# A deformable convolution on one core: window tiles of 4 by 4 pixels become 2 by 8, and five of nine sampling weights travel through DRAM as two factors

## The chip, the cores and the metric

The kernel runs on one core of a Trainium2 chip. The core has a matrix engine (TensorE, PE in the profile), a vector engine (VectorE, DVE), a scalar engine (ScalarE, ACT), a general engine (GpSimd, POOL) and a sequencer that issues transfers (SyncE, SP). Transfers run on sixteen DMA engines that SP and ACT both feed. The metric is the device time of one execution in microseconds (us). Everything is float32.

## The reference

The input is x[2, 128, 128, 128] (image, channel, row, column). Four layers are added up in a residual stream; the third of them is the one that changes. It is a deformable 3 by 3 convolution with 128 input and 128 output channels on the normalised stream g:

```
off, mask = conv3x3(g, w_off) + b_off      # 9 taps: (dy, dx) and sigmoid(mask) for each pixel
py = dy + ky + h - 1 ; px = dx + kx + w - 1
sampled[c, k, h, w] = mask * bilinear(g[c], py, px)     # four neighbours, zero outside
out[o, h, w] = sum_{c,k} w_def[o, c, k] * sampled[c, k, h, w] + b_def[o]
```

A bilinear sample is a sum over window positions (y, x) of `hat(py - y) * hat(px - x) * g[c, y, x]` with `hat(t) = relu(1 - |t|)`. So a sample is a product of a row factor and a column factor, and it can be done as a matrix product of the window's pixels with these weights.

## The kernel before

The program is one long unrolled stream. `program` runs an attention layer (`layer0_prepare`, `layer0_attention`, `layer0_merge`), four recurrent scans (`layer1`), the deformable layer (`layer2`) and a Winograd convolution (`layer3`). The change touches `layer2` alone.

`layer2_offsets` goes over 16 blocks of 16 rows. For each it normalises the stream, computes the 27 offset and mask channels with the matrix engine, turns them so that pixels lie on partitions, and sends them to the DRAM buffer `off`; it also turns the normalised image so that columns lie on partitions and sends it to the DRAM buffer `px`, which has a border of zeros. At the end it tests whether an offset is over 2 in size. If none is, `layer2_windows` runs, and that is the case here.

`layer2_windows` cuts the image into 128 halves: four rows (`RT = 4`) by 64 columns. A half has 16 tiles of 4 by 4 pixels, done in two batches of eight tiles (128 pixels), so there are 256 batches. Here a half, or in the new kernel a strip, is called a pair of batches.

- `load` fetches for each half the window of each tile, 10 by 10 positions, with positions on partitions and channels along the free dimension: `xw[100, 16, 128]`. It takes ten transfers, one for each window row, each to ten partitions, and one more for the offsets `o`. All are issued by SP, and `xw` has four buffers.
- `hats`, `hatted` and `masked` make the row and column hats `d[128 pixels, 2, 18, 10]`: DVE subtracts positions from coordinates, ACT takes the absolute value and the relu, DVE multiplies the row hats with the mask.
- `outer` (DVE) multiplies row and column hats of one batch to `w[128, 9, 10, 10]`. `turn` transposes this on PE, one transpose for each tap, to the PSUM tile `ps_w[100, 9, 128]`, and `turned` (DVE) copies it to `s`, ordered by tile.
- `sample` (PE) multiplies for each of eight tiles the window by the weights of its 9 taps and 16 pixels: 8 products with 144 columns into `ps_s`. `sampled` (ACT) copies this to `sm` with three copies.
- `convolve` (PE) sums nine products of `wdef` with `sm` over the 256 pixels of a half into `po`, five taps in one batch and four in the next. `finish` (DVE) adds `po` and the bias to the stream, and takes the statistics for the next norm after every second half.

Each float32 product runs as two passes on PE, so eight products are 16 matrix instructions in the profile; a transpose is one.

The order is written out by hand. `InOrder` makes PE, DVE and ACT keep the program's order. In iteration `b` of the loop PE does `turn` for batch b+1, `sample` for b, and then the part of `convolve` for the half before; ACT does `sampled` after `sample`. A framework places all waits. It gives every transfer of SP and ACT one of eight semaphores in turn (numbers 100 to 107 in the trace, the two engines share them), and a transfer waits before its issue until the one that last had its semaphore has landed.

Nearly all instructions of the loop are recorded under line 81, the helper `InOrder`; they are told apart by their tiles.

Of the kernel before, what the change touches and what calls it, by code (L numbers as in the profile page):

```python
# [7 lines left out]
F32 = mybir.dt.float32  # L8
# [7 lines left out]
P = 128  # L16
N = 2
# [7 lines left out]
TP = S + 6  # L25
# [1099 lines left out]
def layer2_offsets(env, prm, res, mem, st_gn, far):  # L1125
# [5 lines left out]
    with ExitStack() as ctx:  # L1131
# [7 lines left out]
        zero = cp.tile([P, 402], F32, name="zero", tag="zero")  # L1139
        nc.vector.memset(zero, 0.0)  # L1140
        for n in range(N):
            flat = mem["px"][n].rearrange("y x k -> (y x k)")
            for y in (0, S + 3):
                span = 3 * TP * P
                nc.scalar.dma_start(
                    out=flat[y * TP * P : y * TP * P + span].rearrange("(p k) -> p k", p=P),
                    in_=zero,
                )
            for c in (0, S + 3):
                nc.scalar.dma_start(  # L1150
                    out=mem["px"][n, 3 : S + 3, c : c + 3, :].rearrange("y x k -> y (x k)"),
                    in_=zero[:, 0 : 3 * P],
                )
# [7 lines left out]
        for n in range(N):  # L1161
            for h in range(0, S, NR):
# [15 lines left out]
                for k in range(9):  # L1178
# [9 lines left out]
                om = sp.tile([P, 4, RT, 32], F32, name="om", tag="om")  # L1188
                nc.scalar.activation(
                    om.rearrange("p b r c -> p r b c"),  # L1190
                    ps.rearrange("p r (b c) -> p r b c", b=4),
                    AF.Identity,
                    bias=boff,
                )
# [38 lines left out]
def layer2_windows(env, prm, res, mem, st_next):  # L1233
# [3 lines left out]

    nc, tc = env.nc, env.tc
    ident = env.ident
    with ExitStack() as ctx:  # L1240
# [3 lines left out]
        pe, dve, act = (InOrder(tc, e) for e in (nc.tensor, nc.vector, nc.scalar))  # L1244
# [4 lines left out]
        base = cp.tile([P, 18, 10], F32, name="base", tag="base")  # L1249
        nc.scalar.dma_start(out=base, in_=prm["base2"])  # L1250

        px = mem["px"]
        halves = [(n, g, hf) for n in range(N) for g in range(NT) for hf in range(2)]

        def load(at):
            n, g, hf = halves[at]
            xw = sp.tile([100, 16, P], F32, name="xw", tag="xw", bufs=4)
            for y in range(10):
                here = px[n, g * RT + y, hf * 64 : hf * 64 + 10, :]
                src = bass.AP(  # L1260
                    tensor=here.tensor,
                    offset=here.offset,
                    ap=[[P, 10], [4 * P, 16], [1, P]],
                )
                nc.sync.dma_start(out=xw[10 * y : 10 * y + 10], in_=src)
            o = sp.tile([P, 2, 27], F32, name="o", tag="o", bufs=4)
            nc.sync.dma_start(out=o, in_=mem["off"][n, g, :, 2 * hf : 2 * hf + 2, :])
            return xw, o

        def hats(o):  # L1270
            d = sp.tile([P, 2, 18, 10], F32, name="d", tag="d")
            dve.tensor_tensor(
                d,
                o[:, :, 0:18].unsqueeze(3).to_broadcast([P, 2, 18, 10]),
                base.unsqueeze(1).to_broadcast([P, 2, 18, 10]),
                ALU.add,
            )
            return d

        def hatted(d):  # L1280
            act.activation(d, d, AF.Abs)
            act.activation(d, d, AF.Relu, bias=1.0, scale=-1.0)

        def masked(d, o):
            rows = d.rearrange("p b (k a) s -> p b k a s", a=2)[:, :, :, 0, :]
            dve.tensor_tensor(
                rows, rows, o[:, :, 18:27].unsqueeze(3).to_broadcast([P, 2, 9, 10]), ALU.mult
            )

        def outer(d, b):  # L1290
            w = sp.tile([P, 9, 10, 10], F32, name="w", tag="w")
            v = d[:, b].rearrange("p (k a) s -> p k a s", a=2)
            dve.tensor_tensor(
                w,
                v[:, :, 0, :].unsqueeze(3).to_broadcast([P, 9, 10, 10]),
                v[:, :, 1, :].unsqueeze(2).to_broadcast([P, 9, 10, 10]),
                ALU.mult,
            )
            return w

        def turn(w):
            ps = pp.tile([100, 9, P], F32, name="ps_w", tag="ps_w")
            for k in range(9):
                pe.transpose(ps[:, k, :], w[:, k].rearrange("p y x -> p (y x)"), ident)
            return ps

        def turned(ps):

            s = sp.tile([100, 8, 36, 4], F32, name="s", tag="s")
            dve.tensor_copy(  # L1310
                s.rearrange("p t k c -> p k t c"),
                ps.rearrange("p k (r t c) -> p (k r) t c", r=4, t=8),
            )
            return s

        def sample(xw, s, b):
            ps = pp.tile([P, 3, 512], F32, name="ps_s", tag="ps_s")
            for t in range(8):
                pe.matmul(
                    ps[:, t // 3, (t % 3) * 144 : (t % 3) * 144 + 144],  # L1320
                    lhsT=xw[:, 8 * b + t, :],
                    rhs=s[:, t].rearrange("p k c -> p (k c)"),
                    start=True,
                    stop=True,
                )
            return ps

        def sampled(ps, sm, b):
            for j in range(3):
                nt = (3, 3, 2)[j]  # L1330
                lo = 8 * b + 3 * j
                act.copy(
                    sm.rearrange("p k (t c) -> p k t c", c=4)[:, :, lo : lo + nt, :],
                    ps[:, j, 0 : nt * 144].rearrange("p (t k c) -> p k t c", t=nt, c=4),
                )

        def convolve(sm, po, taps):
            for k in taps:
                pe.matmul(
                    po,  # L1340
                    lhsT=wdef[:, k, :],
                    rhs=sm[:, 4 * k : 4 * k + 4, :],
                    start=(k == 0),
                    stop=(k == 8),
                )

        def finish(at, po):
            n, g, hf = halves[at]
            here = res[n][:, g * RT : g * RT + RT, hf * 64 : hf * 64 + 64]
            dve.scalar_tensor_tensor(here, po, bdef[:, 0:1], here, ALU.add, ALU.add)  # L1350
            if hf == 1:
# [7 lines left out]
        count = len(halves)  # L1359
        loads = {at: load(at) for at in range(3)}  # L1360
        ds = {}
        for at in range(2):
            ds[at] = hats(loads[at][1])
            hatted(ds[at])
            masked(ds[at], loads[at][1])
        w = outer(ds[0], 0)
        ps_w = turn(w)
        s = turned(ps_w)
        w = outer(ds[0], 1)
        sms, pos = {}, {}  # L1370
        for b in range(2 * count + 2):
# [3 lines left out]
            if part == 0 and at < count:  # L1375
                sms[at] = sp.tile([P, 36, 64], F32, name="sm", tag="sm")


            s_now = s
            if b + 1 < 2 * count:  # L1380
                ps_w = turn(w)
                s = turned(ps_w)
                if b + 2 < 2 * count:
                    w = outer(ds[(b + 2) // 2], b % 2)
            if at + 2 < count:
                if part == 0:
                    ds[at + 2] = hats(loads[at + 2][1])
                else:
                    masked(ds[at + 2], loads[at + 2][1])
            if b < 2 * count:  # L1390
                ps_s = sample(loads[at][0], s_now, part)
                sampled(ps_s, sms[at], part)
                if part == 0 and at + 2 < count:
                    hatted(ds[at + 2])
            if at >= 1:
                if part == 0:
                    pos[at - 1] = pp.tile([P, RT, 64], F32, name="po", tag="po_w", bufs=2)
                convolve(sms[at - 1], pos[at - 1], range(0, 5) if part == 0 else range(5, 9))
                if part == 1:
                    finish(at - 1, pos.pop(at - 1))  # L1400
                    sms.pop(at - 1), loads.pop(at - 1), ds.pop(at - 1)
# [336 lines left out]
def program(ctx, tc, prm, out):  # L1738
# [16 lines left out]
    mem["px"] = dram.tile([N, TP, TP, P], F32, name="px_d", tag="px_d")  # L1755
# [21 lines left out]
def constants(np):  # L1777
# [27 lines left out]
    pix = np.arange(P)[:, None, None]  # L1805
    at = np.stack(
        [tap // 3 + 2 + pix[:, 0] // 32, tap % 3 + 2 + pix[:, 0] % 4], 2
    ).reshape(P, 18, 1)
    base2 = (at - np.arange(10)).astype(np.float32)
# [94 lines left out]
```

## Time and profile before

| | |
|---|---|
| three runs | 5779.77, 5784.55 and 5788.11 us, median 5784.55 us |
| profiled execution | 5786.06 us; its span, first to last instruction, 5783.8 us |
| busy in the span | PE 5374.1 us, DVE 3770.7 us, ACT 2638.0 us, POOL 1292.9 us |
| deformable layer, offsets part | 3836 to 4017 us |
| deformable layer, windows part | first load issued at 4024.0 us, first sample 4056.3 us, last addition to the stream ends at 5310.0 us |
| PE busy, 4500 to 5100 us | 600.0 of 600 us, granted clock 1.00 |
| DVE and ACT busy, 4500 to 5100 us | 381.0 and 207.7 us |

A line of the profile names the line of code, the engine, the operation, the tile that is written and those that are read, the number of partitions and elements, and how often it occurs. Then follow busy time and mean duration, and the idle time of the engine just before such instructions with what ended it. Matrix instructions are pipelined: their durations overlap, so the cost of one is the distance between starts. PEld is the loading of weights for the next product, beside PE.

### The profile page before, as it was taken

How to read it: one execution, taken by the hardware profiler on the slowest of the kernel's cores; microseconds unless marked ns; L12 is line 12 of the kernel's file. 1: busy time of each engine (PE TensorE's matmuls, PEld its weight loads, DVE VectorE, ACT ScalarE, POOL GpSimd, SP SyncE). 2: the span in 40 equal slices, each digit the busy share in tenths (PEclk: the TensorE clock that was granted, in tenths of full speed). 3: DMA queues.
4: the chain of work that ended last, by engine and by line, in shares of the span. 5: the costliest groups of instructions: out<-in, count | busy, mean ns of one | idle time of the engine just before them, and what ended most of it. 6: DMA issues, size and time to landing. Idle time of an engine off the chain costs nothing. (4 is left out here: it accounts for less than half of the span.)

```text
span 5783.8 us, 162452 instructions
## 1 busy us (share of the span) xinstructions
PE 5374.1 (93%) x67323; PEld 4833.4 (84%) x67323; DVE 3770.7 (65%) x7273; ACT 2638.0 (46%) x7896; POOL 1292.9 (22%) x983
## 2 busy tenths in 40 slices
PE   8997999999999607999999999997999999998999
PEld 8866888888888407999999999963999999998888
DVE  3645888888888655555555556653666666666887
ACT  1056988899888555442223320012333333333221
POOL 2114666666666420000000013310000000000000
PEclk9998999999999758999999999998999999999999
DMA  3243333333333482000000001114667676773001
GB/s 145 96 190 109 60 58 65 60 59 61 63 60 58 141 316 79 1 2 1 2 1 1 1 9 45 39 60 121 89 88 87 86 87 89 87 90 50 41 37 41
DMA packets 411363, 401.00 MB, mean 69 GB/s; under 512 B 63232, under 2 KB 368256, under 8 KB 397952
## 3 DMA queue, kind: packets, MB, share of 16 engines
q1 hardware_dynamic: 406160, 380.65, 31.5%
q8 instruction: 541, 8.86, 0.7%
q10 hardware_dynamic: 4464, 9.86, 0.5%
q14 instruction: 198, 1.62, 0.1%
HBM read 251.00 MB, written 139.37 MB: 67 GB/s over the span
## 5 line engine op out<-in xcount | busy, mean ns | idle before, releaser
L81 PE MATMUL pl<-ln,wl 128*128 128x128 f32 (+1 forms) x10160 | 1238.5, 276 | 8.1 <-DVE ln L81 8.1
L81 PEld LDWEIGHTS pl<-ln,wl 128*128 128x128 f32 x10160 | 1175.6, 190 | 18.2 <-issue 5.1
L81 ACT ACTIVATE e<-e,mx 128x128 f32<-128x128 f32 x2048 | 793.5, 395 | 1.0 <-DVE mx L81 1.0
L81 ACT COPY sm<-ps_s 128x432 f32<-128x432 f32 (+1 forms) x768 | 318.2, 487 | 797.5 <-PE ps_s L81 797.5
L81 POOL TENSOR_TENSOR e<-e,total 128x1024 f32<-128x1024 f32 x256 | 485.6, 1897 | 481.9 <-DVE total L81 473.6
L81 ACT COPY res<-ln 128x128 f32<-128x128 f32 x762 | 261.8, 344 | 720.5 <-DVE ln L81 720.5
L81 PE MATMUL ps_s<-s,xw 100*128 100x144 f32 x4096 | 545.2, 286 | 0.5 <-ACT sm L81 0.5
L81 DVE COPY s<-ps_w 100x1152 f32<-100x1152 f32 x256 | 346.5, 1353 | 299.8 <-PE ps_w L81 299.8
L81 PE MATMUL po<-sm,wdef 128*128 128x256 f32 x2304 | 539.2, 379 | 0.0
L81 PE MATMUL pl<-ln,ws 128*128 128x128 f32 x4064 | 537.3, 273 | 0.0
L81 POOL COPY et<-et 128x1024 f32<-128x1024 f32 x256 | 518.9, 2027 | 34.9 <-DVE et L81 25.9
L81 PEld LDWEIGHTS ps_s<-s,xw 100*128 100x128 f32 x4096 | 517.2, 190 | 1.1 <-ACT sm L81 1.0
L81 DVE TENSOR_TENSOR v<-pl,c 128x128 f32<-128x128 f32 x508 | 148.2, 292 | 539.5 <-PE pl L81 539.5
L81 PEld LDWEIGHTS pl<-ln,ws 128*128 128x128 f32 x4064 | 495.1, 191 | 0.0
L81 ACT ACTIVATE r<-gen,alphas 128x1536 f32<-128x1536 f32 x256 | 395.0, 1543 | 164.7 <-PE gen L81 140.3
L81 POOL TENSOR_TENSOR res<-ln,x1t 128x128 f32<-128x128 f32 x256 | 134.0, 524 | 1484.4 <-DVE ln L81 1484.4
L81 PEld LDWEIGHTS po<-sm,wdef 128*128 128x128 f32 x2304 | 419.8, 190 | 47.6
L81 PE MATMUL m<-x,weff 128*128 128x256 f32 x2048 | 445.2, 381 | 15.1 <-DVE x L81 15.1
L81 PEld LDWEIGHTS m<-x,weff 128*128 128x128 f32 x2048 | 391.2, 191 | 68.8 <-issue 15.1
L1653 POOL MEMSET col<- 128x10 f32 x32 | 3.7, 116 | 1867.5 <-ACT weff L1633 1488.3
L81 ACT ACTIVATION_READ_ACCUMULATOR e<-e,mx 128x1 f32 x2048 | 396.2, 193 | 0.0
L81 DVE SCALAR_TENSOR_TENSOR ln<-v,res 128x128 f32<-128x128 f32 x1016 | 343.9, 339 | 48.6 <-DVE v L81 0.9
(225 smaller groups left out, 8782.4 us busy)
## 6 DMA issues: line engine op xcount, KB each, us to landing
xw<-px_d SPq DMA_DIRECT2D x1280, 80.0 KB
xa<-in_x SPq DMA_DIRECT2D x16, 1024.0 KB
v_d<-vs SPq DMA_DIRECT2D x16, 1024.0 KB
qb_d<-sb SPq DMA_DIRECT2D x16, 1024.0 KB
qa_d<-sa SPq DMA_DIRECT2D x8, 2048.0 KB
zz<-qb_d SPq DMA_DIRECT2D x1024, 16.0 KB
vt<-v_d SPq DMA_DIRECT2D x64, 256.0 KB
qk<-qa_d SPq DMA_DIRECT2D x256, 64.0 KB
```

The costliest lines, as they stand in the source:

```text
L81: return lambda *a, **k: self.tc.keep_in_program_order(issue(*a, **k))
L1653: nc.gpsimd.memset(cols[0][:, :, 0:1], 0.0)
```

## The change

The windows part takes another cut of the image and another way for the weights of five taps.

- **Tiles.** The 128 units are strips of two rows by 128 columns. A batch is half a strip, 2 by 64 pixels, with eight tiles of 2 by 8 pixels. A window is 8 rows by 16 columns (`WY`, `WX`), so 128 positions (`KW`). `px` gets two more zero columns. The offsets part writes its transposed values in the strip's order, which splits one ACT instruction (`om`) into two.
- **Loads.** A batch's windows come with eight transfers, one for each tile, each to 128 partitions: the four even tiles issued by SP, the four odd tiles by ACT. There are five buffers of one batch each; the loads of batch b+5 are issued after `sampled` of batch b. The offsets are a transfer of their own (`load_offsets`). SP keeps the program's order too.
- **Five taps as factors.** Row and column hats lie in `d` by place (24 places: 8 rows and 16 columns) and tap, five taps first and four after. `hats` takes four DVE instructions and `masked` two. `send` turns the factors of five taps for a whole strip with two transposes (`ps_h`), ACT copies them (`ht`), and SP stores them in a DRAM buffer `hat` with two transfers. `receive` reads them back with two transfers into `hat0` and `hat1`, `[128, 2, 5, 128]` each: the row factors repeated for each of 16 columns, the column factors repeated for each of 8 rows.
- **Four taps as before.** `outer` and `turn` do four taps. `weights` (DVE) fills `s`: a product of `hat0` and `hat1` for five taps, and a copy of `ps_w` for four.
- **Convolution.** `convolve` does all nine taps for 128 pixels of one batch, for the batch before.

```diff
+WX, WY = 16, 8
+KW = WX * WY
+PLACES = WX + WY
+TD = 5
...
+        def load(b):
+            n, g, k = strips[b // 2]
+            y, x = g * RT + 2 * k, b % 2 * 64
+            xw = sp.tile([KW, 8, P], F32, name="xw", tag="xw", bufs=5)
+            for part, queue in enumerate((sync, act)):
+                for t in range(part, 8, 2):
+                    queue.dma_start(
+                        out=xw[:, t, :],
+                        in_=mem["px"][
+                            n, y : y + WY, x + 8 * t : x + 8 * t + WX, :
+                        ].rearrange("y x k -> x y k"),
+                    )
+            return xw
...
+        def send(at, d):
+            ps = pp.tile([PLACES * TD, 2, P], F32, name="ps_h", tag="ps_h")
+            for b in range(2):
+                pe.transpose(ps[:, b, :], d[:, b, 0 : PLACES * TD], ident)
+            ht = sp.tile([PLACES * TD, 2, P], F32, name="ht", tag="ht")
+            act.copy(ht, ps)
+            for b in range(2):
+                sync.dma_start(out=there(at)[:, b], in_=ht[:, b, :])
+
+        def receive(at):
+            got = []
+            src = there(at).rearrange("s b k x -> s (b k x)")
+            for a in range(2):
+                t = sp.tile([KW, 2, TD, P], F32, name=f"hat{a}", tag=f"hat{a}")
+                here = src[0:WY] if a == 0 else src[WY:PLACES]
+                dims = [list(v) for v in here.ap]
+                dims = [[0, WX], dims[0], dims[1]] if a == 0 else [dims[0], [0, WY], dims[1]]
+                sync.dma_start(
+                    out=t.rearrange("p b k x -> p (b k x)"),
+                    in_=bass.AP(tensor=here.tensor, offset=here.offset, ap=dims),
+                )
+                got.append(t)
+            return got
...
+        def weights(got, b, ps):
+            s = sp.tile([KW, 8, 18, 8], F32, name="s", tag="s")
+            to = s.rearrange("p t k c -> p k t c")
+            row, col = (
+                t[:, b].rearrange("p k (r t c) -> p (k r) t c", r=2, t=8) for t in got
+            )
+            dve.tensor_tensor(to[:, 0 : 2 * TD], row, col, ALU.mult)
             dve.tensor_copy(
...
+                to[:, 2 * TD : 18], ps.rearrange("p k (r t c) -> p (k r) t c", r=2, t=8)
             )
             return s
...
+        for b in range(2 * count + 1):
             at, part = b // 2, b % 2
-            if part == 0 and at + 3 < count:
-                loads[at + 3] = load(at + 3)
...
+            if part == 0 and at + 4 < count:
+                offs[at + 4] = load_offsets(at + 4)
             s_now = s
             if b + 1 < 2 * count:
-                ps_w = turn(w)
-                s = turned(ps_w)
+                s = weights(gots[(b + 1) // 2], 1 - part, turn(w))
                 if b + 2 < 2 * count:
-                    w = outer(ds[(b + 2) // 2], b % 2)
...
+                    w = outer(ds[(b + 2) // 2], part)
+            if part == 0 and at + 2 < count:
+                send(at + 2, ds[at + 2])
+            if part == 0 and at + 3 < count:
+                ds[at + 3] = hats(offs[at + 3])
+            if part == 1 and at + 3 < count:
+                masked(ds[at + 3], offs.pop(at + 3))
             if b < 2 * count:
-                ps_s = sample(loads[at][0], s_now, part)
-                sampled(ps_s, sms[at], part)
...
+                ps_s = sample(xws[b], s_now)
+                sms[b] = sampled(ps_s)
+                if part == 0 and at + 3 < count:
+                    hatted(ds[at + 3])
+            if part == 1 and at + 2 < count:
+                gots[at + 2] = receive(at + 2)
+            if b + 5 < 2 * count:
+                xws[b + 5] = load(b + 5)
+            if b >= 1:
+                last, half = (b - 1) // 2, (b - 1) % 2
+                if half == 0:
+                    pos[last] = pp.tile([P, 2, S], F32, name="po", tag="po_w", bufs=2)
+                convolve(sms.pop(b - 1), pos[last][:, :, 64 * half : 64 * half + 64])
+                if half == 1:
+                    finish(last, pos.pop(last))
```

More of the change, by code (lines that the diff above doesn't have):

```diff
@@ L1248, in layer2_windows @@
         nc.scalar.dma_start(out=bdef, in_=prm["bdef"])
-        base = cp.tile([P, 18, 10], F32, name="base", tag="base")
+        base = cp.tile([P, 9 * PLACES], F32, name="base", tag="base")
         nc.scalar.dma_start(out=base, in_=prm["base2"])
[L1252 to L1268, printed above, removed]
@@ L1270, in hats @@
-        def hats(o):
[L1271 to L1277, printed above, removed]
+        hat = mem["hat"]
+        strips = [(n, g, k) for n in range(N) for g in range(NT) for k in range(2)]
+        count = len(strips)
+        def load(b):
[11 more added lines that the diff above has]
+            return xw
@@ new lines, in load_offsets, with parts @@
+        def load_offsets(at):
+            n, g, k = strips[at]
+            o = sp.tile([P, 2, 27], F32, name="o", tag="o", bufs=3)
+            sync.dma_start(out=o, in_=mem["off"][n, g, :, 2 * k : 2 * k + 2, :])
+            return o
+        def parts(t):
+            cut = PLACES * TD
+            return (
+                (t[..., 0:cut].rearrange("... (s k) -> ... s k", k=TD), slice(0, TD)),
+                (t[..., cut:].rearrange("... (s k) -> ... s k", k=TT), slice(TD, 9)),
+            )
@@ new lines, in hats @@
+        def hats(o):
+            d = sp.tile([P, 2, 9 * PLACES], F32, name="d", tag="d", bufs=3)
+            for (to, taps), (less, _) in zip(parts(d), parts(base)):
+                for a, here in ((0, slice(0, WY)), (1, slice(WY, PLACES))):
+                    out = to[:, :, here, :]
+                    dve.tensor_tensor(
+                        out,
+                        o[:, :, a:18:2][:, :, taps].unsqueeze(2).to_broadcast(list(out.shape)),
+                        less[:, here, :].unsqueeze(1).to_broadcast(list(out.shape)),
+                        ALU.add,
+                    )
@@ L1284, in masked, with there @@
         def masked(d, o):
[L1285 to L1288, printed above, removed]
+            for to, taps in parts(d):
+                rows = to[:, :, 0:WY, :]
+                mask = o[:, :, 18:27][:, :, taps].unsqueeze(2).to_broadcast(list(rows.shape))
+                dve.tensor_tensor(rows, rows, mask, ALU.mult)
+        def there(at):
+            n, g, k = strips[at]
+            return hat[:, n * NT + g, 2 * k : 2 * k + 2]
@@ L1347, in finish @@
         def finish(at, po):
[L1348 to L1349 removed]
+            n, g, k = strips[at]
+            here = res[n][:, g * RT + 2 * k : g * RT + 2 * k + 2, :]
             dve.scalar_tensor_tensor(here, po, bdef[:, 0:1], here, ALU.add, ALU.add)
[L1351 removed]
+            if k == 1:
                 dve.bn_stats(
@@ L1355, in finish @@
                 )
-        count = len(halves)
-        loads = {at: load(at) for at in range(3)}
-        ds = {}
+        offs, ds, gots, xws, sms, pos = {}, {}, {}, {}, {}, {}
+        for at in range(3):
+            offs[at] = load_offsets(at)
+        xws[0] = load(0)
+        for at in range(3):
+            ds[at] = hats(offs[at])
+            hatted(ds[at])
+            masked(ds[at], offs.pop(at))
+            if at < 2:
+                send(at, ds[at])
+        offs[3] = load_offsets(3)
@@ L1362, in layer2_windows @@
         for at in range(2):
-            ds[at] = hats(loads[at][1])
-            hatted(ds[at])
-            masked(ds[at], loads[at][1])
+            gots[at] = receive(at)
+        for b in range(1, 5):
+            xws[b] = load(b)
         w = outer(ds[0], 0)
-        ps_w = turn(w)
-        s = turned(ps_w)
+        s = weights(gots[0], 0, turn(w))
         w = outer(ds[0], 1)
-        sms, pos = {}, {}
-        for b in range(2 * count + 2):
+        for b in range(2 * count + 1):
             at, part = b // 2, b % 2
-            if part == 0 and at + 3 < count:
-                loads[at + 3] = load(at + 3)
-            if part == 0 and at < count:
-                sms[at] = sp.tile([P, 36, 64], F32, name="sm", tag="sm")
+            if part == 0 and at + 4 < count:
+                offs[at + 4] = load_offsets(at + 4)
```

106 lines of the change are left out of this document (48 added, 58 removed).

## The prediction

> **What bounds the kernel now.** I read the busy shares first, then the windows part by stretches, then PE's order of work in it, and last what SP's transfers wait for. The stretches (length, then busy time of PE, PEld, DVE, ACT and POOL, then clock, DMA share and GB/s):
>
> ```profile
> 4500.00:4700.00 200.00, 200.00 (x1394) 187.83 (x1393) 126.69 (x153) 69.16 (x164) 0.00 (x0) 1.00 0.67 87
> 4700.00:4900.00 200.00, 200.00 (x1394) 187.76 (x1393) 127.36 (x154) 68.88 (x164) 0.00 (x0) 1.00 0.71 88
> ```
>
> PE is never idle and its clock is full. A pair of batches has 68 matrix instructions (2 x (9 + 16 + 9)), so a pair takes 200 / 1394 x 68 = 9.76 us, and 128 pairs are 1249 us. In order of time:
>
> ```profile
> 4700.17 1.15 PE L81 MATMUL ps_w<-cst_main,w 128*100 128x128 f32 x9
> 4701.15 2.13 PE L81 MATMUL ps_s<-s,xw 100*128 100x144 f32 x16
> 4703.11 2.32 PE L81 MATMUL po<-sm,wdef 128*128 128x256 f32 x10
> 4705.27 1.15 PE L81 MATMUL ps_w<-cst_main,w 128*100 128x128 f32 x9
> ```
>
> The distance between starts is the price: 0.98 us for 9 transposes (109 ns each), 1.96 us for 16 passes of 144 columns (122.5 ns), 2.16 us for 10 passes of 256 (216 ns). What the other engines do, 4300 to 5200 us:
>
> ```profile
> L81 DVE COPY s<-ps_w 100x1152 f32<-100x1152 f32 x184 | 249.0, 1353 | 214.4 <-PE ps_w L81 214.4
> L81 DVE TENSOR_TENSOR w<-d 128x900 f32<-128x900 f32 x184 | 199.8, 1086 | 0.0
> L81 ACT COPY sm<-ps_s 128x432 f32<-128x432 f32 x368 | 173.0, 522 | 570.0 <-PE ps_s L81 570.0
> L81 ACT ACTIVATE d<-d 128x360 f32<-128x360 f32 x184 | 94.5, 514 | 18.3 <-DVE d L81 15.4
> ```
>
> DVE and ACT wait for PE. SP's waits, for the whole run (us in all, times, longest):
>
> ```profile
> SPq L1265 <- PE ps_s L81: 386.9, 115, 5.0
> SPq L1265 <- DMA xw<-px_d: 227.7, 406, 1.4
> ...
> SPq L1265 <- DMA wdef<-in_wdef: 3.2, 1, 3.2
> ```
>
> The first is a buffer coming free. The others are transfers that wait for a transfer with which they share no data: the eight shared semaphores. The third shows that SP waits so for one that ACT issued. Today this costs nothing, because the loads run three halves ahead.
>
> **What the change takes from PE.** Per batch 9 transposes become 4, and `send` adds 2 per strip, so 1: 5 x 109 = 0.55 us for 0.98. `sample` stays 16 x 122.5 = 1.96. `convolve` becomes 18 passes of 128 columns for 9 of 256; the scans' products of that shape start 109 to 112 ns apart, so 1.96 to 2.02 us for 1.94. Together 4.47 to 4.53 us; I take 4.52, or 9.04 a pair. If PE stayed the bound, 128 x (9.76 - 9.04) = 92 us would go. The `pl` rows already show 128 by 128 weights loaded anew for each pass of 128 columns at that distance, so the load lies hidden beside the stream. The Trainium skill ("TensorE: Matmul & The Clock Gate", The mechanism, and LDWEIGHTS) speaks against this half of the change: a weight load overlaps a running product only in another row group, and 128 columns take 128 / 1.2 = 107 ns. By it nine loads more per batch would cost an estimated 0.96 us, 246 us in all, and turn the gain of 92 into a loss of some 154.
>
> **DVE, per pair**, at the rows' 1.04 ns an element plus 0.15 us (900 elements 1.09 us, 360 elements 0.53 us): `outer` 2 x 0.68 for 2 x 1.09; `weights` 2 x (640 elements, 0.82, and a PSUM copy of 512, 0.69 as such a copy takes elsewhere) for 2 x 1.35; `hats` four instructions on 432 elements 1.05 for 0.53; `masked` two, 0.45 for 0.34; `finish` and statistics stay at 0.83. That is 6.7 us beside 9: hidden. Without that cover it would be 0.1 us a pair more than now (6.6).
>
> **ACT, per pair:** the `sampled` copies 2 x 1.24 as now, `hatted` 2 x 0.58 for 432 elements (0.51 for 360), the `ht` copy 0.36 (as 128x256 from PSUM elsewhere), and eight transfers. ACT's transfers of zeros took 0.33 to 0.47 us each to issue: 3.2 us. Sum 7.2 of 9: it fits, but ACT's next copies queue behind each issue, and PE's next `sample` behind these copies (one `ps_s`). The `om` split costs 0.03 us a block: nothing.
>
> **SP, per pair:** thirteen issues (offsets, 2 sends, 2 receives, 8 loads) at 0.40 us, the distance of back-to-back loads now: 5.2 us. The loads move from the head of the iteration to behind `sampled`; being five batches ahead, some 22 us, they are not late by that. POOL issues nothing in this part.
>
> **DMA, per pair.** Now a load goes to ten partitions, and its semaphore gets eleven steps where a transfer to 128 partitions gets sixteen; its 512-byte packets take 53 ns in the median, 27 at best. 1600 of them at about 190 per us, the rate in the first loads, need 8.4 of the 9.76 us. After: 2048 packets of 512 bytes over 16 engines (128 each), 256 of 5,120 bytes (16 each), 240 to `hat`, 128 of offsets. At 27 ns, which the sends of `px` from all 128 partitions also show (28), and 198 ns (4,608 bytes take 178): 128 x 0.027 + 16 x 0.198 + 20 x 0.028 + 0.2 = 7.4 us of 9. At 53 ns for the loads it is 10.7. I take 27 ns as the partitions are those of the sends, and keep 53 for the range. The skill ("DMA: Bandwidth & Descriptors", Why a DMA increments its semaphore by 16 and not by 1) reads the eleven steps as ten engines, by the outer dimensions, and would give the new loads sixteen; it sets no price for a packet, so the sum by it is the same.
>
> **The new round trip.** This decides. Between `receive` of one strip and `send` of the next the program has 13 transfers (12 loads and the offsets), more than the eight semaphores. So one of them waits until `receive` has landed; whether SP or ACT issues it, the next `send` stands behind it (on ACT its `ht` copy does). And `receive` waits for `send` to land, as it reads those bytes. The strips' transfers form one chain, however far ahead `receive` is written. One turn, from the landing of `receive` (0):
>
> - The held load starts at once (17 ns after a landing in this trace), then offsets, first send, second send start at 0.4 us steps: second send at 1.2.
> - It lands 1.9 to 2.4 us later (`sve_d` stores, also 64 KB in 512-byte rows: least 1.87, median 2.37, issue to last semaphore step): 3.1 to 3.6.
> - SP must also issue the next batch's four loads, the first of which wants the semaphore of the held load: about 2.2 (64 KB), plus 4 x 0.4 = 3.8. So `receive` starts at 3.8.
> - Its two reads are 1.31 MB. The nearest single reads: 590 KB (`wl`) land in 3.7 us, 1.05 MB (`x1t`) in 5.1, and the second half adds 8 x 0.198 = 1.6: 5.4 us. Meanwhile ACT's four loads, freed when the sends and two loads land, share the engines: 4 x 8 x 27 ns = 0.85.
> - Sum 3.8 + 5.4 + 0.85 = 10.05 us a pair. Ends: 8.9 (stores 1.9, nothing shared) and 10.9 (everything at its slower row), and 12 if the repeated reads run at 300 GB/s with 53 ns loads beside them.
>
> This is above PE's 9.04 and above today's 9.76, so PE will wait. I take 10.05: 128 x 0.29 = +37 us.
>
> The skill's first fixed cost for a transfer ("DMA: Bandwidth & Descriptors", Anatomy of one DMA) is about 2.0 us plus bytes at 436 GB/s, measured on another queue. By it the turn would be an estimated 3.8 + 5.0 + 0.85 = 9.65, and the change a gain of 24 us with the start.
>
> **Start and end.** PE's first sample comes 32 us after the first load now, since three halves of loads go first. Afterwards: base lands near 4031, hats, relu and mask 2.7, transposes and copy 0.7, sends 2.8, `receive` 5.4, weights 1.5: near 4045. I take 10 us saved; 0 and 13 are the bounds.
>
> **Sum** against the profiled execution's 5786 us (span 5784 and 2 around it, 1.5 above the runs' median): 5786 - 10 + 37 = 5813.
>
> **Rivals.**
>
> 1. *The round trip hides.* If `receive` lands within 5.2 us of its start, sharing included, a turn is 9.04 or less and PE bounds: 5786 - 10 - 92 = 5684. For it: 27 ns packets and a DMA sum of 7.4. Against: no read of 1 MB in this trace landed faster than 4.9. The sign turns at a turn of 9.84 us. Between lies a half gain: through ACT, whose loads wait for the sends and whose copies PE needs, I count 9.4 (send 2.6, loads issued to 5.6, landed 8.5, issue and `ht` copy 0.9): 5786 - 10 - 46 = 5730.
> 2. *DMA becomes the bound.* Packets of 512 bytes stay at 53 ns: 10.7 us of engine time, a turn near 11: 5786 - 10 + 159 = 5935. For it: that is today's median; against: ten partitions explain it.
> 3. *The repeated reads don't use sixteen engines.* On eight, 256 packets of 5,120 bytes take 6.3 us for 3.2, a turn of 13.2: 5786 - 10 + 440 = 6216. Against: the outer dimension is 16 in both.
>
> **How the numbers follow.** Turn 9.7 to 10.6 (5770 to 5885): 0.43. Rival 1 whole: 0.20; half: 0.17. Rival 2: 0.16. Rival 3: 0.04. About 0.2%, 12 us, is what a measurement can tell from no change. Faster is rival 1 and its half, and a little of the first: 0.38; within 0.2% is a turn of 9.75 to 9.93: 0.08; slower 0.54. The range runs from PE's floor, 5682, to 5925, short of rival 2's middle; the likeliest case alone has 5770 to 5885.
>
> **What would show it.** Right: PE with 1 us idle per pair in the windows part, ended by the DVE product that waits for `hat0` or `hat1` from DMA, or by `sm`; SP's loads waiting for `hat0` or `hat1` to land; sends waiting behind; first sample near 4045. Wrong: PE busy through (rival 1); packets of 512 bytes at 50 ns and DMA share near 1 (rival 2); fewer than 16 steps of the receives' semaphores (rival 3). What breaks the forecast most easily is the 5.4 us of two repeated reads, which nothing in this trace resembles.

## The result, and the profile after

The changed kernel takes 6377.3 us (median of 4 runs, 6372.5 to 6383.5), against 5782.2 us before on the same chip: a ratio of 1.1028, 95% interval 1.1009 to 1.1047. It is 10% slower. The forecast was 5813 us and its range ended at 5925: the direction was right, the size was not. The profiled execution has a span of 6373.4 us.

The stretches of the windows part, in the columns of the same view before (length, busy time of PE, PEld, DVE, ACT, POOL, then clock, DMA share, GB/s):

```profile
4300.00:4500.00 200.00, 152.18 (x1098) 149.93 (x1098) 92.59 (x191) 54.34 (x126) 0.00 (x0) 0.86 0.75 176
4700.00:4900.00 200.00, 154.40 (x1078) 152.33 (x1079) 91.67 (x189) 54.34 (x126) 0.00 (x0) 0.85 0.75 174
```

PE was busy for all of the 200 us; now it idles for some 46 of them, and its clock is no longer full. A pair of batches has 78 matrix instructions now (2 x (4 + 1 + 16 + 18)), and the turn, the distance from one strip's `receive` to the next, is 14.43 us in the median. Forecast was 10.05; before, a pair took 9.76. PE in order of time (start, duration, what; in brackets the idle time ahead and what ended it):

```profile
5001.19 2.13 PE L86 MATMUL ps_s<-s,xw 128*128 128x144 f32 x16
5003.15 2.17 PE L86 MATMUL po<-sm,wdef 128*128 128x128 f32 x18
5009.05 1.09 PE L86 MATMUL ps_w<-cst_main,w 128*128 128x128 f32 x4 [3.72 <-DVE d L86]
5009.93 0.63 PE L86 MATMUL ps_h<-cst_main,d 128*120 128x128 f32 x2
5010.35 4.05 PE L86 MATMUL ps_s<-s,xw 128*128 128x144 f32 x16
...
5023.34 0.63 PE L86 MATMUL ps_w<-cst_main,w 128*128 128x128 f32 x4 [2.26 <-DVE d L86]
5023.80 0.38 PE L86 MATMUL ps_h<-cst_main,d 128*120 128x128 f32 x2
5024.02 2.13 PE L86 MATMUL ps_s<-s,xw 128*128 128x144 f32 x16
```

The passes themselves have the forecast's prices: 1.96 us from the start of 16 passes to the next group. What is new are the gaps at the head of a turn, and after the longer one (3.72 us) the passes run at half speed for a while: 16 of them took 4.05 us, and 2.13 after the gap of 2.26. DVE is named as the releaser, but it is late itself, as the second row below shows. What DVE, PE and ACT wait for, 4300 to 5300 us (us in all, times, longest):

```profile
ACT sm L86 <- DMA xw<-px_d: 351.3, 61, 8.4
DVE s L86 <- DMA hat<-hat_d: 309.4, 68, 7.5
...
PE ps_w L86 <- DVE d L86: 245.7, 69, 6.4
...
ACT ht L86 <- DMA xw<-px_d: 180.7, 57, 4.2
```

The second row is a real need: the product that makes `s` wants the hats read back. The first and fourth are not. ACT's copies need no `xw`; they stand behind ACT's own loads, which wait for a semaphore, as ACT in order of time shows:

```profile
5016.18 5.11 ACTq L86 DMA_DIRECT2D xw<-px_d  x4
5021.33 0.52 ACT L86 COPY sm<-ps_s 128x432 f32<-128x432 f32 x1 [4.60 <-DMA xw<-px_d]
```

SP's waits in that stretch (4300 to 5300 us) say the same, the second row once a turn (69 times, 2.5 us each):

```profile
SPq L86 <- DMA xw<-px_d: 224.7, 140, 3.8
SPq L86 <- DMA hat<-hat_d: 171.7, 69, 3.7
```

One turn on SP in order of time (start, duration of all the issues of the row, what, how many):

```profile
5020.94 0.33 SPq L86 DMA_DIRECT2D o<-off_d  x1
5021.59 1.64 SPq L86 DMA_DIRECT2D hat_d<-ht  x2
5023.34 2.49 SPq L86 DMA_DIRECT2D xw<-px_d  x4
5025.94 1.17 SPq L86 DMA_DIRECT2D hat<-hat_d  x2
5027.22 6.35 SPq L86 DMA_DIRECT2D xw<-px_d  x4
```

The `receive` before had landed at 5020.72, and only then does the row of offsets start. The semaphores of the trace tell what held it, the same in all 69 turns from 4300 to 5300 us. SP's fourth load waits for the first read of the `receive`, and ACT's next load for the second. The offsets wait for neither: they want the semaphore of the window load that SP issued 0.7 us behind the second read, and this load lands 0.25 us after that read (medians). What is to be sent, `ht`, had by then been ready for 9 us or more. So the sends wait for semaphores, and not for data.

The two sends take 0.8 us each to issue, the four loads 0.62 each; the next `receive` starts 5.2 us after the landing of the last, and lands at 5035.40, 9.5 us later.

The medians of the turns, without some twenty at the start and ten at the end, make a ledger of two terms:

| from the landing of a `receive` | forecast, us | measured, us |
|---|---|---|
| second send starts | 1.2 | 1.93 |
| second send has landed | 3.1 to 3.6 | 4.25 |
| next `receive` starts | 3.8 | 5.84 |
| the pair of reads, issue to landing | 6.25 | 8.49 |
| turn | 10.05 | 14.43 |

(The medians add up to 14.33; they are taken one by one.) 128 x (14.43 - 9.76) = 598 us, and the start saves 6 (the first `sample` is at 4050.0 us, before at 4056.3): 5786 - 6 + 598 = 6378, against 6375 in the profiled execution. The whole loss lies in the turn. What is to be explained is why both terms are so much longer than forecast.

### The profile page after: what moved, and what is told of

Same layout as the page of the kernel before. It is cut to its first block, busy times and chain, and to the rows that moved or that the text cites. A ratio compares the mean times of both kernels' runs of the same rounds, so it can differ in the third digit from the quotient of the medians.

```text
span 6373.4 us, 167224 instructions
## 1 busy us (share of the span) xinstructions
PE 5519.6 (87%) x68603; PEld 5036.6 (79%) x68603; DVE 3818.5 (60%) x8041; ACT 2701.6 (42%) x8040; POOL 1293.0 (20%) x983
## 5 line engine op out<-in xcount | busy, mean ns | idle before, releaser
L86 PE MATMUL ps_s<-s,xw 128*128 128x144 f32 x4096 | 703.9, 339 | 7.1 <-ACT sm L86 7.1
L86 PEld LDWEIGHTS ps_s<-s,xw 128*128 128x128 f32 x4096 | 680.9, 240 | 7.4 <-ACT sm L86 7.4
L86 PE MATMUL ps_w<-cst_main,w 128*128 128x128 f32 x1024 | 194.5, 323 | 459.4 <-DVE d L86 440.2
L86 PE MATMUL po<-sm,wdef 128*128 128x128 f32 x4608 | 564.5, 277 | 0.0
L86 DVE TENSOR_TENSOR s<-hat,hat 128x640 f32<-128x640 f32 x256 | 211.2, 825 | 584.8 <-DMA hat<-hat_d 565.2
L86 PEld LDWEIGHTS po<-sm,wdef 128*128 128x128 f32 x4608 | 550.6, 195 | 0.0
L86 PEld LDWEIGHTS ps_w<-cst_main,w 128*128 128x128 f32 x1024 | 137.0, 164 | 480.5 <-issue 477.2
```

The costliest lines, as they stand in the source:

```text
L86: return lambda *a, **k: self.tc.keep_in_program_order(issue(*a, **k))
```

## The experiments

The kernel before took 5784 to 5790 us on the chips of these runs. "Landing to next" and "pair" are the two terms of the ledger, in medians of the same turns.

**Which part costs?** The first two runs take the round trip away, with and without the five taps' savings on PE.

Sends and receives for the first two strips alone; the hats are still turned and copied:

```diff
-            for b in range(2):
-                sync.dma_start(out=there(at)[:, b], in_=ht[:, b, :])
+            if at < 2:
+                for b in range(2):
+                    sync.dma_start(out=there(at)[:, b], in_=ht[:, b, :])
...
-                gots[at + 2] = receive(at + 2)
+                gots[at + 2] = gots[at]
```

> Only the first two strips are sent and received; later strips use their factors again, so the weights of five taps are those of other pixels. The transposes and the ht copies stay, four transfers per pair are left out. Theory (the chain through receive and send bounds the part): no chain is left, PE bounds at 9.04 us a pair, 5680 to 5740 us. Rival (ACT's issuing of loads, or the loads themselves, hold PE): over 6000 us.

Measured: 5698.3 us.

```profile
4700.00:4900.00 200.00, 200.00 (x1730) 199.97 (x1729) 145.05 (x297) 86.68 (x202) 0.00 (x0) 1.00 0.43 120
```

PE is busy throughout, at 200 / 1730 x 78 = 9.02 us a pair; ACT still issues its four loads a batch, and PE isn't held up by it. So the new PE work costs what was forecast (9.04), and everything above 5698 us is the round trip with its reads.

The tiles of 2 by 8 and the loads to 128 partitions alone, all nine taps turned on PE:

```diff
-TD = 5
+TD = 0
...
-            if at < 2:
-                send(at, ds[at])
...
-            if part == 1 and at + 2 < count:
-                gots[at + 2] = receive(at + 2)
```

> The tiles of 2 by 8 pixels with their loads on both queues alone: all nine taps are made by outer, turned by nine transposes and copied; send, receive and the factors are left out. Complete computation. Theory: PE bounds at 2 x (9 x 0.109 + 1.96 + 2.0) = 9.9 us a pair, 5770 to 5830 us. Rival (ACT's issuing of loads holds PE): over 6000 us.

Measured: 5804.8 us, PE busy for 600 of 600 us with 5185 instructions, 600 / 5185 x 86 = 9.95 us a pair. The new tiles and loads by themselves hold nothing up and gain nothing.

**Why does the pair of reads take 8.5 us?** In the changed kernel the packets of 512 bytes have a median of 27 ns, as forecast, but those of 5,120 bytes 369 ns (10% at 196, 90% at 404), where 198 was forecast. Three suspects: the places lie 640 KiB apart in DRAM; each place is read 8 or 16 times; the bytes were written a few us before.

The places of a strip 5 KB apart:

```diff
-    mem["hat"] = dram.tile([PLACES, N * NT, 4, TD, P], F32, ...)
+    mem["hat"] = dram.tile([N * NT, 2, PLACES, 2, TD, P], F32, ...)
...
-            return hat[:, n * NT + g, 2 * k : 2 * k + 2]
+            return hat[n * NT + g, k]
```

> One edit: the buffer hat is laid out strip by strip, so that the 24 places of a strip lie 5 KB apart instead of 640 KiB. Theory (one chain per strip: receive lands, the next send, the next receive; its receives are slow in this kernel because their 5,120-byte packets take 369 ns in the median instead of 196). If the distance of the places is what makes them slow: packets near 200 ns, receive pair lands in 5.4 to 6.3 us instead of 8.5, a turn falls from 14.4 to 11.3 to 12.2 us, 5980 to 6095 us in all. If the repetition of the same bytes is what makes them slow: packets stay near 370 ns, and 6350 to 6400 us. Rival (the loads that ACT issues hold its copies and so PE, whatever receive does): 6350 to 6400 us.

Measured: 6336.7 us, a turn of 13.97, landing to next 5.67, pair 8.18, packets of 5,120 bytes 364 ns. The pitch is worth some 41 us of the 595 lost. The Trainium skill ("DMA: Bandwidth & Descriptors", Latency and other measured facts) tells of large power-of-two row pitches, which at 4 MiB cut the rate to about half, with an inferred cause. The pitch here, 640 KiB, is no power of two, and this run shows that another pitch leaves most of the slowness in place (364 ns for 369).

The same number and size of packets to the same partitions, but every partition reads bytes of its own, in `px`:

```diff
-                    in_=bass.AP(tensor=here.tensor, offset=here.offset, ap=dims),
+                    in_=px[lo : lo + KW * 2 * TD * P].rearrange("(p k) -> p k", p=KW),
```

> The two receives read as many bytes in as many packets of 5,120 bytes, but 128 different rows of the buffer px that lie one behind the other, so nothing is repeated; the weights of five taps are then wrong. The sends stay. receive no longer waits for send by its data, but stands behind it on SP all the same. Theory, repeated reads slow: packets near 196 ns, receives land in 5.4 to 6.3 us, a turn of 11.3 to 12.2 us, 5980 to 6095 us. Rival (the volume of the receives beside the loads is what costs, whatever they read): packets stay over 300 ns, 6300 to 6400 us.

Measured: 6112.5 us, just above the theory's range, a turn of 12.28, landing to next 5.43, pair 6.51, packets of 196 ns. This pair is near the forecast's 6.25. But these bytes were also old. So the repetition was put back, still reading old bytes of `px`:

```diff
-                    in_=px[lo : lo + KW * 2 * TD * P].rearrange("(p k) -> p k", p=KW),
+                    in_=bass.AP(tensor=here.tensor, offset=here.offset, ap=dims),
```

Here `here` is 8 or 16 rows of `px`, and `dims` repeats them as in the changed kernel.

> As the run whose receives read different bytes for every partition, with the repetition put back: the receives read the same old tensor px, eight places for 16 partitions each and 16 places for eight partitions each, in the pattern of the changed kernel (the five taps' weights are not theirs). It parts two things that the other run changed at once: there no byte was read twice, and none had been written a few us before. Theory (the repetition itself is slow): 5,120-byte packets of 330 to 380 ns, the pair of receives lands 8.2 us after its issue, a turn of 14.0, near the 6337 us of the buffer laid out strip by strip. Rival (bytes written just before are slow to read, repetition costs nothing): packets of 196 ns, 6.5 us, a turn of 12.3, near 6112 us.

Measured: 6351.1 us, a turn of 14.17, pair 8.28, packets of 365 ns. The repetition is the cause, and the age of the bytes is not. Both reads are slow: of the 256 packets of a turn the first 128 to start, mostly those of the eight rows read by 16 partitions each, take 339 ns in the median, and the others, mostly those of the 16 rows read by eight, 376.

**Why does the next `receive` start 5.8 us after a landing?** The first theory was the one of the forecast: the tie lies in the semaphores that sends and receives share with the loads. So GpSimd, which is idle here and has semaphores of its own, was made to issue them:

```diff
-                sync.dma_start(out=there(at)[:, b], in_=ht[:, b, :])
+                pool.dma_start(out=there(at)[:, b], in_=ht[:, b, :])
...
-                sync.dma_start(
+                pool.dma_start(
                     out=t.rearrange("p b k x -> p (b k x)"),
```

> Sends and receives are issued by GpSimd, idle in this part, whose transfers have eight semaphores of their own; nothing else changes. Theory (the eight semaphores that SP and ACT share tie each send to the landing of the receive before it): the chain is cut, and receives run ahead. What bounds then is PE at 9.04 us a pair or the DMA engines at 16 x 0.37 + 128 x 0.027 + 0.8 = 10.2 us, so 5690 to 5880 us, by the sum 5830. Rival (the repeated reads themselves, or the loads behind them in the same rings, bound a pair): over 6150 us.

Measured: 6305.6 us, a turn of 13.92, landing to next 5.26, pair 8.97. Only 72 us went; the theory fell in this form. The waits of that run, 4300 to 5300 us:

```profile
POOL hat_d L86 <- ACT ht L86: 582.9, 71, 12.1
ACT ht L86 <- DMA xw<-px_d: 284.3, 38, 9.7
```

and SP's own:

```profile
SPq L86 <- DMA xw<-px_d: 422.7, 104, 7.0
```

The send waits for ACT's copy `ht`, and this stands behind ACT's loads. A load that has the DMA engines to itself lands 2.2 us after its issue; one that meets a `receive` lands with it. In this run a quarter of SP's and of ACT's loads take over 7.6 us, and one in twenty over 9.1, though the `receive` is issued by another engine. Eight such loads fill the eight semaphores, SP and ACT stop, and the chain closes again through the loads. The Trainium skill ("DMA: Bandwidth & Descriptors", Issuing engines are not separate DMA queues) has transfers of all issuing engines interleave on the same DMA engines, and says that another issuer saves only the sequencer's time, usually little beside the transfer. The first half agrees with the 2.2 and 7.6 us here. The second did not hold in the run further on that moves four of a batch's eight loads from ACT: 348 us went.

The same with fewer taps as factors, so that the reads are shorter and PE's own pair longer:

```diff
-TD = 5
+TD = 4
```

> As the run with sends and receives on GpSimd, but four taps go as factors and five are turned. Theory: packets of 4,096 bytes near 0.30 us, DMA engines 16 x 0.30 + 3.5 + 0.8 = 9.1 us, PE 2 x (6 x 0.109 + 1.96 + 2.0) = 9.24 us a pair: PE bounds, 5710 to 5780 us. Rival (repeated reads bound): over 6000 us.

Measured: 6073.8 us, a turn of 11.91, landing to next 4.00, pair 7.82.

```diff
-TD = 5
+TD = 3
```

> As the run with sends and receives on GpSimd, but three taps go as factors and six are turned. Theory: DMA engines 7.9 us, PE 2 x (7 x 0.109 + 1.96 + 2.0) = 9.45 us a pair: PE bounds, 5735 to 5790 us. Rival (repeated reads bound): over 5900 us.

Measured: 5915.7 us, a turn of 10.75, landing to next 4.10, pair 6.59. Both missed, most likely for the same reason as the run with five. The terms shrink with the reads, but from 4300 to 5300 us the sends still wait for `ht` for 542 and 528 us, and SP for its loads for 396 and 338 us.

If ACT is where the chain closes, its loads must go elsewhere. SP keeps sends and receives, GpSimd takes ACT's four loads a batch:

```diff
-            for part, queue in enumerate((sync, act)):
+            for part, queue in enumerate((sync, pool)):
```

> The loads that ACT issues are issued by GpSimd; sends and receives stay on SP. Then SP's semaphores see five transfers, not thirteen, between a receive and the next send, and the send is no longer held by the receive; held is the first load after the sends, and the next receive stands behind four loads. Theory: a turn is those 2.4 us and 8.5 us for the receives, about 11 us, 5900 to 6050 us. Rival (the chain is one of data alone, send to receive, or of ring order on SP): 6300 us and more. Rival (ACT's issuing holds PE): under 5750 us.

Measured: 6029.1 us, a turn of 11.61, as expected. 348 us went with one word, and all of it from one term: landing to next fell from 5.84 to 2.92, the pair stayed (8.57). SP in order of time shows how:

```profile
5003.41 1.16 SPq L86 DMA_DIRECT2D hat<-hat_d  x2
5004.74 2.55 SPq L86 DMA_DIRECT2D xw<-px_d  x4
5007.33 0.59 SPq L86 DMA_DIRECT2D o<-off_d  x1
5008.03 2.25 SPq L86 DMA_DIRECT2D hat_d<-ht  x2
5012.35 2.89 SPq L86 DMA_DIRECT2D xw<-px_d  x4
5015.46 1.16 SPq L86 DMA_DIRECT2D hat<-hat_d  x2
```

With SP almost alone on the eight semaphores, the two reads, four loads, the offsets and the first send take all eight. The sends now go out from 5008.03 on, while the `receive` is still in flight; the second one waits for the first read (landed 5009.48). The transfer that is held until the second read has landed (5012.27) is the first of the next four loads, at 5012.35. So only these four issues lie between landing and next `receive`, and beside them the landing of the second send, at 5015.38.

The move does two things: SP's transfers have the eight semaphores almost to themselves, and ACT's copies no longer stand behind loads. As `ht` lay ready 9 us ahead in the changed kernel, the first is what the send there lacked. It also changes the packets: GpSimd's loads show as packets of 4,096 bytes where ACT's have 512. But 512- and 4,096-byte packets together take 4.5 us of the sixteen engines a turn, against 4.6 in the changed kernel, so the gain isn't theirs. What is left is nearly all transfer:

```profile
4300.00:4500.00 200.00, 169.03 (x1334) 166.09 (x1332) 113.13 (x233) 66.15 (x154) 72.11 (x139) 0.94 0.92 219
```

The DMA engines are busy for 0.92 of the time, 10.7 us of the 11.61. In the changed kernel it was 0.75 of 14.43, 10.8 us, while a pair took 9.76 us before the change. So by this estimate, and if the packets keep their price, five taps with repeated reads stay slower than the kernel before in any order of issue.

**Both causes together.** First with five taps: distinct bytes, and ACT's loads on GpSimd (the edits of both runs).

> Five taps, as the changed kernel, but both suspected causes taken away at once: the receives read different bytes for every partition (the same number, size and destination of packets, no byte read twice, so the five taps' weights are not theirs) and ACT's loads are issued by GpSimd. Theory (the two causes add): 2.9 us from landing to next receive plus 6.5 us of transfer = 9.4 us, a little above PE's 9.04: 5786 - 10 - 128 x 0.36 = 5730 us. Rival (there is a third cause, such as the DMA engines themselves being full with both kinds of transfer): a turn of 10.5 or more, 5870 us or more.

Measured: 5832.4 us, a turn of 10.10, landing to next 2.67, pair 7.16. Between the two expectations, and nearer the rival's 10.5: the first term is there, but the pair took 7.16 us and not the 6.51 it took with ACT's loads in their old place. The packets are again 196 ns; the DMA share rose from 0.67 to 0.86, since the loads of a turn now meet the reads in 10.1 us and not in 12.3. So a third cause, most likely the sharing of the DMA engines, grows as the turn shrinks, and the two gains don't quite add: 265 + 348 us were to go, 545 went.

Then as kernels that compute everything: ACT's loads on GpSimd, the strip-by-strip layout, and four taps or three.

```diff
-TD = 5
+TD = 4
...
-            for part, queue in enumerate((sync, act)):
+            for part, queue in enumerate((sync, pool)):
...
-            return hat[:, n * NT + g, 2 * k : 2 * k + 2]
+            return hat[n * NT + g, k]
```

> The same with four taps turned as factors. Theory: 2.9 + 7.8 - 0.3 = 10.4 us a turn, above PE's 9.2, so the round trip bounds: 5786 - 10 + 128 x 0.64 = 5858 us. Rival (the chain forms again through the loads): 11.6 us a turn as with five taps, 6010 us or more.

Measured: 5859.3 us, where the sum of the two terms had said 5858. A turn is 10.36 us, landing to next 2.75, pair 7.27; these are 10.02, so part of the agreement is luck.

The same with `TD = 3`:

> Three taps turned as factors instead of five, ACT's loads issued by GpSimd, and the buffer in DRAM laid out strip by strip. Theory (a turn is the stretch from a landed receive to the start of the next, 2.9 us as with ACT's loads on GpSimd, plus the transfer of the receive, 6.6 us as with three taps in GpSimd's hands, less 0.3 for the layout): 9.2 us, just under PE's own 9.41 (14 transposes x 109 ns, 32 x 122.5 ns, 36 x 110 ns). PE bounds again: 5786 - 10 - 128 x 0.35 = 5731 us, faster than before. Rival (the chain forms again elsewhere, through loads that land late beside the receive and hold the eight semaphores, as in the two runs with fewer taps, which gave 1.3 to 1.5 us a pair more than the sum said): a turn of 10.5, 5870 us.

Measured: 5774.5 us (median of 10 runs, 5769.6 to 5778.4) against 5783.9: a ratio of 0.9983, interval 0.9974 to 0.9993. It is faster than the kernel before by 9 us, 0.2%, which the interval only just tells from no change, and not by the 53 that the theory gave.

```profile
4700.00:4900.00 200.00, 196.74 (x1690) 195.22 (x1690) 156.34 (x280) 79.93 (x186) 86.25 (x166) 1.00 0.81 202
```

PE is busy for 98% at full clock, 196.74 / 1690 x 82 = 9.55 us a pair and not 9.41, and a turn takes 9.71 (landing to next 3.08, pair 6.41, together 9.49). That is 0.16 us above the larger of its two limits. That limits so close together cost some of each other is a likely reading, and no run tests it.

The two terms of all runs, in us:

| run | landing to next | pair | turn | time |
|---|---|---|---|---|
| changed kernel | 5.84 | 8.49 | 14.43 | 6377 |
| old bytes, repeated | 5.72 | 8.28 | 14.17 | 6351 |
| strip by strip | 5.67 | 8.18 | 13.97 | 6337 |
| sends, receives on GpSimd | 5.26 | 8.97 | 13.92 | 6306 |
| distinct bytes | 5.43 | 6.51 | 12.28 | 6113 |
| GpSimd, four taps | 4.00 | 7.82 | 11.91 | 6074 |
| ACT's loads on GpSimd | 2.92 | 8.57 | 11.61 | 6029 |
| GpSimd, three taps | 4.10 | 6.59 | 10.75 | 5916 |
| loads on GpSimd, four taps, strip by strip | 2.75 | 7.27 | 10.36 | 5859 |
| loads on GpSimd, distinct bytes | 2.67 | 7.16 | 10.10 | 5832 |
| loads on GpSimd, three taps, strip by strip | 3.08 | 6.41 | 9.71 | 5774 |

In every row the two terms make up the turn to within 0.4 us.

## Why the prediction was right and wrong

- **PE, "4.52, or 9.04 a pair": right.** Without the round trip a pair takes 9.02 us. The weight loads lie hidden beside the stream, as the `pl` rows had said; the 246 us that the page's rule would have added are not there.
- **DVE, "6.7 us beside 9": right.** 92 of 200 us busy in a turn of 14.43 are 6.65 us.
- **The chain: right in its effect, and only in part in its path.** "One of them waits until `receive` has landed" is in the trace, on SP and on ACT, and so are the signs named: PE idle at the head of a turn, DVE's product waiting for the hats, SP for their landing. But the last thing that holds the offsets, and with them the sends, is a window load. The text let the held load land in 2.2 us; the loads that stand behind a `receive` land only with it. With semaphores of their own, sends and receives still met such loads, and only 72 us went. Nor does the landing of the send set the start of the next `receive`, as the next point shows.
- **"At 0.4 us steps" and "4 x 0.4 = 3.8": the first step that failed.** The 3.8 were eight issues at 0.4 us and 0.6 us of waiting for the held load. The 0.4 is the distance of the old window loads. Measured are 0.33 us for the offsets, 0.80 for a send, and for a new window load 0.60 on SP and 0.53 on ACT, so the seven issues ahead of the next `receive` take 4.3 us. Some 1.2 us lie between them, mostly waits for the semaphores of window loads: 0.30 us a turn ahead of the offsets, 0.55 ahead of the sends, 0.18 ahead of the `receive` (means). So it starts at 5.84 and not at 3.8, long after the send's landing at 4.25. Worth 2.0 us a turn, 261 us. With these issues SP's sum is 7.9 us (8 x 0.60 + 2 x 0.80 + 2 x 0.60 + 0.33) where "5.2 us" stood.
- **"5.4 us" and "8 x 0.198" for the two reads: the second step that failed.** The price of a packet was taken from reads in which no byte is read twice; repeated, the packets take 369 ns. 16 engines need 3.0 us for each of the two reads where 1.6 was reckoned, and the pair takes 8.49 us, not 6.25. Worth 2.2 us a turn, 287 us. The distinct read, at 196 ns and 6.51 us, shows that the rest of the step was sound. The text named this as the easiest to break, and bounded it at 300 GB/s for the reads; measured were 1.31 MB in 6.3 us of transfer, 208 GB/s. One reading beside it, held against rival 1, was off: reads of 1 MB had landed faster than "4.9", four of `tv` in 4.7 us.
- **"128 x 27 ns": right** for the median packet of 512 bytes; rival 2, with 53, is refuted. But the engines' sum, "7.4 us of 9", came out at 10.8, and 2.6 of the 3.4 are the repeated reads. Rival 3 gave the nearest time (6216) by a mechanism that isn't there: the receives' semaphores get 16 steps.
- **"10 us saved" at the start: 6.**
- **The range** failed too. It ended short of rival 2 and held no case in which both disputed terms went wrong at once, though each rested on rows of another shape. Both did.

## What to carry to other kernels

When a round trip through DRAM sits in a loop, write the turn as a sum, landing to next issue plus issue to landing, and price both with rows of the same shape: the issue by a transfer of the same access pattern, the read by whether its bytes are read again. Count which transfer stands on the semaphore that the slow one holds, and what is queued behind it on that engine: here one word that moved four loads to an idle issuer was worth 348 us of the 595 lost. Then add up the engines that the detour uses: here the DMA engines' 10.8 us a turn stood above the 9.76 that were to be beaten. A detour that saves an engine 7% has little room: with three taps both limits lay under 9.76, and 9 us were gained.

## What the runs showed of the hardware

- Reading the same bytes again is slow: packets of 5,120 bytes take 196 ns when each is read once and 364 to 369 when each is read by 8 or 16 partitions, at a pitch of 640 KiB or of 5 KB, and written just before or long before. Why was not found.
- The time of an issue depends on the transfer, and not on its partitions alone: offsets to 128 partitions take 0.33 us, a window load to 128 takes 0.60 (0.53 on ACT), a send from 120 takes 0.80, and the old window loads to ten lay 0.40 apart. What in the access pattern sets it was not tested.
- The same window load shows as 128 packets of 512 bytes when SP or ACT issues it, and as 16 packets of 4,096 bytes when GpSimd does, at 206 ns each in the median.
- A 64 KB load that lands in 2.2 us alone can take 7 to 9 us when it meets a 1.3 MB read, also when the two are issued by different engines.
- After an idle time of 3.72 us PE ran 16 passes in 4.05 us instead of 2.13; the granted clock of the stretch from 4700 to 4900 us was 0.85. How much of that lies on the chain wasn't measured.
- Not tried: `receive` written ahead of the four loads on SP. In the changed kernel it could then start when the send has landed, at 4.25 us and not at 5.84.
